# A third attention head transposed in squares by VectorE, with its stores and buffers rearranged

## The chip, the core and the metric

The kernel runs on one core of a Trainium2 chip. The metric is the device time of one execution in microseconds (us). A core has TensorE (PE, matrix products; its weight loads are PEld), VectorE (DVE), ScalarE (ACT), GpSimd (POOL) and SyncE (SP), each with its own instruction queue in program order. They wait for one another by semaphores. Data moves between main memory, the on-chip memory SBUF and within SBUF by DMA; nearly all transfers of this kernel are issued by SP. TensorE writes to PSUM, the accumulators.

## What is computed

A gated block on 8 sequences of 512 tokens with 512 features: cross attention with 16 heads of 32, then a mixture of 8 experts of which each token takes two, up to 615 tokens an expert. Everything is float32. Cut to what matters:

```python
# x, ctx: (8, 512, 512)
Q = proj(layernorm(x), Wq, bq); K = proj(ctx, Wk, bk); V = proj(ctx, Wv, bv)
attn = softmax(Q @ K^T / sqrt(32))                 # per sequence and head, 512 x 512
x = x + tanh(g_xattn) * ((attn @ V) @ Wo.T + bo)
probs = softmax(layernorm(x) @ Wr + br)            # 8 experts
gates, ids = top_k(probs, 2)
# each expert: its tokens in order of gate, 615 at most
h = silu(xg @ W1 + b1); y = (h @ W2 + b2) * gate
x = x + tanh(g_ffn) * scatter_add(y)
```

The change touches the attention stage only; the expert stage comes after it.

## The kernel before

The attention stage walks over *units* (b, c, qc): batch b (8 sequences), c (4 groups of four heads, for 4 x 32 = 128 rows), and qc (4 tiles of 128 queries). There are 128 units. Four units with the same b and c are called a group here, and the sixteen units of a batch have positions 0 to 15.

A unit is a softmax over 4 heads x 128 queries x 512 keys. `scores` makes the four score tiles in PSUM (`s`, L352) and VectorE takes their maxima (`nm`, L361). `soften` lets ScalarE take the exponentials (L375), which sum themselves. The product with V needs the probabilities with the keys on the partitions, so each head's 128x512 tile has to be transposed. This is done in two ways. Two heads (0 and 1, tile `pr`) are transposed by TensorE, four 128x128 transposes a head (L236, in `turned`), and ScalarE copies the result from PSUM to `p_t` (L395). The other two (2 and 3, tile `by_part`) are first moved by four DMAs a unit, one for each block of 32 key positions (L380), into the tile `laid_p`; there VectorE transposes 32x32 squares straight into `p_t` (L405, in `turn_laid_heads`).

The loop over units is a hand-made pipeline, and every engine keeps its written order (the scheduler is manual):

```python
for n, u in enumerate(units):
    loads(b, c, qc)
    ps, nm = scores(nxt)
    # pre: norms' statistics and rows, routing steps
    # at qc == 0: weighted(previous c), the product with V
    turn_heads(u)
    soften(nxt, ps, nm)
    # main: one projection; at qc == 0: divide
    # more: turning of rows, router
    turn_laid_heads(u)
```

So in the iteration of unit u the scores of the next unit come first, then the TensorE transposes of u, the exponentials and laid transfers of the next unit, one projection (q at qc 0, k at 1, v of the next batch at 2, the output projection of the batch before at 3; `pj`, L300), and VectorE's squares of u come last. `weighted` (L423, `po`) needs all four heads' `p_t` of the four units; `divide` (L442, `o_t`) multiplies `po` by the reciprocal sums, which TensorE spreads (`pt_r`, L436) and ScalarE copies (`over`, L438).

The tables `pre`, `main` and `more` put the work of the norms and the router at fixed positions (`put`, `put_ln2`). `ln1_stats`, `ln1_apply` and `ln1_turn` prepare a tile of 128 tokens of the next batch: `bn_stats` on VectorE, the normalized rows `xn` (L229), and their transposition. `ln2_stats`, `ln2_apply` and `ln2_turn` do it for the second norm, after the output projection. `ln2_apply` also issues the stores of the token tile: its residual rows to `out_x` (L261) and its normalized rows to `xn_rows` (L262), from which the experts gather. As `pre` stands ahead of `soften`, these two stores stand ahead of that iteration's four laid transfers in SP's queue.

The pools decide how many tiles of a name are alive: `xn` has 3 buffers, the token tiles `x_1` (first norm) and `x_2` (residual) have 4 each, `by_part`, `laid_p`, `pr` have 2. The two score tiles of a unit use all of the score buffers, so the scores of the unit after next wait for the exponentials of the next one.

## Time and profile before

| what | value |
|---|---|
| time, median of 3 executions | 2032.08 us (2031.86 to 2032.39) |
| the profiled execution | 2030.15 us |
| its span, first to last instruction | 2028.4 us |
| mean granted TensorE clock in it | 0.977 of full speed |

By stretches of that execution:

| stretch (us) | what runs | PE busy | DVE busy | ACT busy | PE clock | DMA share |
|---|---|---|---|---|---|---|
| 0 to 29 | loads, first projections | 29.00 | 8.26 | 7.24 | 1.00 | 0.83 |
| 29 to 142 | batch 0 | 105.41 | 65.78 | 69.92 | 0.97 | 0.40 |
| 142 to 851 | batches 1 to 6 | 697.00 | 470.93 | 446.10 | 1.00 | 0.41 |
| 851 to 967 | most of batch 7 | 109.96 | 72.00 | 68.00 | 0.91 | 0.35 |
| 967 to 1080 | end of attention, first routing | 76.18 | 73.99 | 23.45 | 0.79 | 0.33 |
| 1080 to 2028 | experts | 923.70 | 589.64 | 238.82 | 0.99 | 0.43 |

How to read such views. A row of a group of instructions gives the line, engine, operation, the tiles (written <- read) and shapes, how often it ran, its busy time in total and the mean of one in ns, and the idle time of its engine just before it with what ended that idle time. A timeline gives start and length of merged instructions in order of time. Matmuls are recorded twice here (a float32 product of 512 columns appears as two records), and their ends are modelled. The granted clock is what the chip's throttle let TensorE have.

### The profile page before, as it was taken

How to read it: one execution, taken by the hardware profiler on the slowest of the kernel's cores; microseconds unless marked ns; L12 is line 12 of the kernel's file. 1: busy time of each engine (PE TensorE's matmuls, PEld its weight loads, DVE VectorE, ACT ScalarE, POOL GpSimd, SP SyncE). 2: the span in 40 equal slices, each digit the busy share in tenths (PEclk: the TensorE clock that was granted, in tenths of full speed). 3: DMA queues.
4: the chain of work that ended last, by engine and by line, in shares of the span. 5: the costliest groups of instructions: out<-in, count | busy, mean ns of one | idle time of the engine just before them, and what ended most of it. 6: DMA issues, size and time to landing. Idle time of an engine off the chain costs nothing.

```text
span 2028.4 us, 27201 instructions
## 1 busy us (share of the span) xinstructions
PE 1930.5 (95%) x8784; PEld 1151.1 (57%) x8784; DVE 1279.6 (63%) x2693; ACT 851.8 (42%) x2014; POOL 603.5 (30%) x798
## 2 busy tenths in 40 slices
PE   7989999999999999998669999999999999999997
PEld 3334444444444444444346777777777777777775
DVE  3566666667666666766568675776767667772540
ACT  3656667566666756565213032230403223041321
POOL 1001110010111001110135463536545365464533
PEclk9999999999999999998779999999999999999998
DMA  7243434434343443333511545344553534455332
GB/s 259 74 116 90 128 110 120 125 94 139 104 123 110 121 124 96 103 114 89 150 51 52 157 88 135 89 114 117 110 148 87 138 89 111 124 113 136 88 68 26
DMA packets 291678, 224.58 MB, mean 111 GB/s; under 512 B 26768, under 2 KB 260944, under 8 KB 291536
## 3 DMA queue, kind: packets, MB, share of 16 engines
q1 hardware_dynamic: 282704, 201.96, 35.7%
q0 software_dynamic: 8832, 20.88, 5.6%
q8 instruction: 71, 1.16, 0.3%
q14 instruction: 71, 0.58, 0.1%
HBM read 107.75 MB, written 29.77 MB: 68 GB/s over the span
## 4 chain that ended last, share of the span: by engine, by line
PE 73%; DVE 8%; ACT 7%; DMA 4%; issue 4%; SPq 2%; POOL 1%; POOLq 0%; ACTq 0%; DVEq 0%
PE ps L933 40%; PE pj L300 13%; PE po L423 6%; PE s L352 6%; PE pt L236 5%; ACT by_part L375 3%; DVE nm L361 2%; ACT pr L375 2%; DMA laid_p<-by_part 2%; DVE p_t L405 1%; DMA w<-in_W 1%; SPq L874 1%; SPq L380 1%; DVE ht L917 1%; ACT q_t L309 1%
## 5 line engine op out<-in xcount | busy, mean ns | idle before, releaser
L361 DVE TENSOR_REDUCE nm<-s 128x2 f32<-128x1024 f32 x256 | 298.1, 1204 | 52.6 <-PE s L352 52.5
L395 ACT COPY p_t<-pt 128x512 f32<-128x512 f32 x256 | 138.1, 589 | 276.7 <-PE pt L236 276.5
L933 PE MATMUL ps<-xg_t,w 128*128 128x308 f32 x768 | 220.1, 423 | 0.5 <-ACT u L986 0.5
L223 POOL TENSOR_TENSOR rstd<-rstd,nhalf 128x1 f32<-128x1 f32 x64 | 37.0, 578 | 613.9 <-DVE rstd L222 613.9
L352 PE MATMUL s<-k_t,q_t 32*128 32x512 f32 x1024 | 193.9, 653 | 25.4 <-ACT by_part L375 17.8
L933 PE MATMUL ps<-h,w 128*128 128x308 f32 x768 | 207.5, 425 | 0.0
L375 ACT ACTIVATE by_part<-s,nm 128x512 f32<-128x512 f32 x256 | 174.5, 691 | 53.1 <-DVE nm L361 47.8
L933 PEld LDWEIGHTS ps<-xg_t,w 128*128 128x128 f32 x768 | 145.8, 190 | 53.9 <-ACT u L986 1.0
L375 ACT ACTIVATE pr<-s,nm 128x512 f32<-128x512 f32 x256 | 174.4, 697 | 0.0
L933 PEld LDWEIGHTS ps<-h,w 128*128 128x128 f32 x768 | 143.7, 190 | 52.6 <-issue 3.2
L236 PEld LDWEIGHTS pt<-ident,pr 128*128 128x128 f32 x1024 | 112.5, 143 | 103.4 <-issue 100.3
L405 DVE STREAM_TRANSPOSE p_t<-laid_p 128x512 f32<-128x512 f32 x256 | 165.9, 686 | 5.0 <-DMA laid_p<-by_part 4.7
L933 PE MATMUL ps<-tg,s1w 128*128 128x308 f32 x512 | 145.3, 426 | 9.3 <-ACT p1s L961 5.5
L442 DVE TENSOR_TENSOR o_t<-po,over 128x512 f32<-128x512 f32 x32 | 22.1, 691 | 207.3 <-ACT over L438 207.3
L236 PE MATMUL pt<-ident,pr 128*128 128x128 f32 x1024 | 143.4, 284 | 2.7 <-ACT pr L375 2.7
L423 PE MATMUL po<-p_t,v_s 128*32 128x512 f32 x1024 | 142.4, 628 | 0.9 <-DVE p_t L405 0.9
L933 PE MATMUL ps<-ht,s2w 128*128 128x308 f32 x512 | 137.9, 426 | 0.0
L957 ACT ACTIVATE h<-c,b 128x308 f32<-128x308 f32 x192 | 101.4, 549 | 74.3 <-DVE c L996 72.1
L933 PEld LDWEIGHTS ps<-tg,s1w 128*128 128x128 f32 x512 | 94.9, 190 | 52.8 <-issue 20.5
L300 PE MATMUL pj<-ctx_t,wk 128*128 128x512 f32 x256 | 117.0, 600 | 7.1 <-DMA ctx_t<-in_ctx_t 7.1
L933 PEld LDWEIGHTS ps<-ht,s2w 128*128 128x128 f32 x512 | 95.5, 190 | 34.8 <-issue 1.8
L300 PE MATMUL pj<-xn_t,wq 128*128 128x512 f32 x248 | 111.6, 592 | 0.0
(191 smaller groups left out, 3105.0 us busy)
## 6 DMA issues: line engine op xcount, KB each, us to landing
laid_p<-by_part SPq DMA_DIRECT2D x512, 128.0 KB
w<-in_W SPq DMA_DIRECT2D x128, 256.0 KB
w<-in_W SPq DMA_DIRECT2D x64, 512.0 KB
x<-in_x SPq DMA_DIRECT2D x64, 256.0 KB
laid<-xg SPq DMA_DIRECT2D x140, 64.0 KB
out_x<-x SPq DMA_DIRECT2D x32, 256.0 KB
xn_rows<-xn SPq DMA_DIRECT2D x32, 256.0 KB
ctx_t<-in_ctx_t SPq DMA_DIRECT2D x28, 256.0 KB
```

Of the source, the lines that this page charges most:

```text
L223: nc.gpsimd.tensor_tensor(rstd, rstd, nhalf, ALU.pow)
L236: nc.tensor.transpose(pt[:, c, :], src[:, c * P : (c + 1) * P], ident)
L300: nc.tensor.matmul(ps, lhsT=lhs(ic), rhs=rhs(ic), start=(ic == 0), stop=(ic == DC - 1))
L352: nc.tensor.matmul(ps[i // 2][:, i % 2, :], lhsT=q_t[b, c][r, cols(qc)], rhs=k_t[b, c][r, :], start=True, stop=True,)
L361: nc.vector.tensor_reduce(nm[:, 2 * i : 2 * i + 2], ps[i], AX.X, ALU.max, negate=True)
L375: nc.scalar.activation(to, of, AF.Exp, bias=nm[:, i : i + 1], accum_out=sums[b, c][:, qc, i : i + 1])
L395: nc.scalar.copy(p_t[b, c][i][:, :, cols(qc)].rearrange("p c (q j) -> p c q j", q=DC), pt.rearrange("p c (j q) -> p c q j", q=DC),)
L405: nc.vector.transpose(p_t[b, c][i][:, :, cols(qc)].rearrange("p c (q j) -> p q c j", q=DC), laid[:, :, i - 2].rearrange("p q (c i) -> p q ...
L423: nc.tensor.matmul(po[i * HD : (i + 1) * HD, :], lhsT=v_s[b][:, kc, h * HD : (h + 1) * HD], rhs=pts[i][:, kc, :], start=(kc == 0), stop=(k ...
L442: nc.vector.tensor_tensor(o_t[b][:, c, :], po, over, ALU.mult)
L933: nc.tensor.matmul(ps, lhsT=lhs[k], rhs=rhs[k], start=(k == 0 and not onto), stop=(k == n - 1), skip_group_check=onto,)
L957: nc.scalar.activation(hh[q, i], src, AF.Silu, bias=b1[:, j : j + 1])
```

## The change

It does three things. The second head of `pr` joins the laid path: `by_part` and `laid_p` carry three heads (LH = 3), `pr` one, the exponentials run in the order 2, 3, 1, 0, and VectorE transposes three heads a unit. The two stores of a token tile leave `ln2_apply` and become `ln2_store`, put into `more` at the same position, so after `soften`. And room is made: `xn` has 2 buffers for 3 and `x_1` has 3 for 4; the fourth `x_1` tile of a batch is loaded three units later, and in the first batch it takes an `x_2` buffer.

```diff
+LH = 3
...
-        def load_x(b, j, use):
-            t = acts.tile([P, D], F32, tag=f"x_{use}", name=f"x_{use}", bufs=4)
+        def load_x(b, j, use, of=None):
+            of = of or use
+            t = acts.tile([P, D], F32, tag=f"x_{of}", name=f"x_{of}", bufs=2 + of)
...
-            xn = probs.tile([P, D], F32, tag="xn", name="xn", bufs=3)
+            xn = probs.tile([P, D], F32, tag="xn", name="xn", bufs=2)
...
         def ln2_apply(b, j):
-            t = b * TT + j
             xn = norm_apply((2, b, j))
-            nc.sync.dma_start(out=out[t * P : (t + 1) * P, :], in_=x_in.pop((2, b, j)))
-            nc.sync.dma_start(out=xn_rows[t * P : (t + 1) * P, :D], in_=xn)
             rows_n[2, b, j] = xn
+
+        def ln2_store(b, j):
+            r = slice((b * TT + j) * P, (b * TT + j + 1) * P)
+            nc.sync.dma_start(out=out[r, :], in_=x_in.pop((2, b, j)))
+            nc.sync.dma_start(out=xn_rows[r, :D], in_=rows_n[2, b, j])
...
-            by_part = probs.tile([P, DC, 2, P], F32, tag="by_part", name="by_part")
-            p_sb[u] = probs.tile([P, 2, S], F32, tag="pr", name="pr")
-            for i in (2, 3, 0, 1):
+            by_part = probs.tile([P, DC, LH, P], F32, tag="by_part", name="by_part")
+            p_sb[u] = probs.tile([P, S], F32, tag="pr", name="pr")
+            for i in (2, 3, 1, 0):
...
-            laid_p[u] = probs.tile([P, DC, 2, P], F32, tag="laid_p", name="laid_p")
+            laid_p[u] = probs.tile([P, DC, LH, P], F32, tag="laid_p", name="laid_p")
...
-            pr = p_sb.pop(u)
-            for i in range(2):
-                pt = turned(pr[:, i, :])
-                nc.scalar.copy(
-                    p_t[b, c][i][:, :, cols(qc)].rearrange("p c (q j) -> p c q j", q=DC),
-                    pt.rearrange("p c (j q) -> p c q j", q=DC),
-                )
+            pt = turned(p_sb.pop(u))
+            nc.scalar.copy(
+                p_t[b, c][0][:, :, cols(qc)].rearrange("p c (q j) -> p c q j", q=DC),
+                pt.rearrange("p c (j q) -> p c q j", q=DC),
+            )
...
-            for i in range(2, QH):
+            for i in range(LH):
                 nc.vector.transpose(
-                    p_t[b, c][i][:, :, cols(qc)].rearrange("p c (q j) -> p q c j", q=DC),
-                    laid[:, :, i - 2].rearrange("p q (c i) -> p q c i", c=DC),
+                    p_t[b, c][1 + i][:, :, cols(qc)].rearrange("p c (q j) -> p q c j", q=DC),
+                    laid[:, :, i].rearrange("p q (c i) -> p q c i", c=DC),
                 )
...
             put(pre, b_at, t + 2, ln2_apply, b, j)
+            put(more, b_at, t + 2, ln2_store, b, j)
...
+            if (c, qc) == (0, 3) and b + 1 < B:
+                load_x(b + 1, 3, 1)
...
                 if b + 1 < B and c == 0:
-                    for j in range(2, TT):
-                        load_x(b + 1, j, 1)
+                    load_x(b + 1, 2, 1)
...
             for j in range(TT):
-                load_x(0, j, 1)
+                load_x(0, j, 1, 1 + j // 3)
```

## The prediction

> **What bounds the kernel now.** I read the page's busy times first, then TensorE's clock and busy time by stretches, then the timeline of one group of four units queue by queue, then the waits of VectorE and of SP. On the page, TensorE is busy almost throughout; the three rows that the change moves work between stand below it. Columns are: busy time in total, mean of one in ns, idle time before it.
>
> ```profile
> PE 1930.5 (95%) x8784; PEld 1151.1 (57%) x8784; DVE 1279.6 (63%) x2693; ACT 851.8 (42%) x2014; POOL 603.5 (30%) x798
> ...
> L395 ACT COPY p_t<-pt 128x512 f32<-128x512 f32 x256 | 138.1, 589 | 276.7 <-PE pt L236 276.5
> ...
> L405 DVE STREAM_TRANSPOSE p_t<-laid_p 128x512 f32<-128x512 f32 x256 | 165.9, 686 | 5.0 <-DMA laid_p<-by_part 4.7
> ...
> L236 PE MATMUL pt<-ident,pr 128*128 128x128 f32 x1024 | 143.4, 284 | 2.7 <-ACT pr L375 2.7
> ```
>
> The share of 95% tempts one to price the change as TensorE work saved. The timeline shows that two places of each group are not TensorE's. It is one group (c=0 of batch 4), TensorE, VectorE and ScalarE; columns are start and length in us, then idle time before it.
>
> ```profile
> 503.00 1.20 PE L352 MATMUL s<-k_t,q_t 32*128 32x512 f32 x8
> 504.13 4.62 PE L423 MATMUL po<-p_t,v_s 128*32 128x512 f32 x32
> 508.68 1.09 PE L236 MATMUL pt<-ident,pr 128*128 128x128 f32 x8
> 509.61 3.60 PE L300 MATMUL pj<-xn_t,wq 128*128 128x512 f32 x8
> ...
> 513.58 1.14 PE L352 MATMUL s<-k_t,q_t 32*128 32x512 f32 x8
> ...
> 519.48 1.13 PE L352 MATMUL s<-k_t,q_t 32*128 32x512 f32 x4 [0.30 <-ACT by_part L375]
> 520.81 1.13 PE L352 MATMUL s<-k_t,q_t 32*128 32x512 f32 x4 [0.21 <-ACT pr L375]
> ...
> 526.77 1.14 PE L352 MATMUL s<-k_t,q_t 32*128 32x512 f32 x8
> ...
> 503.78 1.29 DVE L405 STREAM_TRANSPOSE p_t<-laid_p 128x512 f32<-128x512 f32 x2
> ...
> 514.88 0.69 DVE L442 TENSOR_TENSOR o_t<-po,over 128x512 f32<-128x512 f32 x1 [6.40 <-ACT over L438]
> 515.49 1.29 DVE L405 STREAM_TRANSPOSE p_t<-laid_p 128x512 f32<-128x512 f32 x2
> 516.71 2.32 DVE L361 TENSOR_REDUCE nm<-s 128x2 f32<-128x1024 f32 x2
> ...
> 517.98 0.69 ACT L375 ACTIVATE by_part<-s,nm 128x512 f32<-128x512 f32 x1 [1.56 <-DVE nm L361]
> ```
>
> First place: po started at 504.13 and took 4.62; another (534.97 to 538.54, not shown) takes 3.57. The extra 1.05 is head 3's square transposes, which VectorE starts only at 503.78, after it has emptied the projection. Second place: the scores at 519.48 waited, and their second half at 520.81 waited again. Followed back: exps from 517.98, maxima from 516.71, transposes from 515.49, o_t from 514.88. So the periods between scores are 10.58, 5.90, 7.29 and 7.13 us (starts 503.00, 513.58, 519.48, 526.77, 533.90; the last holds 1.0 of the router).
>
> The clock by stretches (us, PE, PEld, DVE, ACT and POOL busy, granted clock, DMA share, GB/s): a stretch with only 1.68 of 3.50 us busy is followed by one at half clock; the emptiest steady stretch, 2.89 busy, is not.
>
> ```profile
> 85.00:88.50 3.50, 1.68 (x10) 0.61 (x8) 2.82 (x4) 3.17 (x10) 0.00 (x0) 1.00 0.07 24
> 89.10:92.50 3.40, 3.40 (x18) 0.78 (x20) 2.52 (x3) 0.00 (x0) 0.00 (x0) 0.50 0.47 101
> 518.80:522.20 3.40, 2.89 (x12) 0.93 (x12) 3.13 (x8) 2.54 (x7) 0.55 (x1) 1.00 0.42 153
> ```
>
> And the waits of VectorE and SP (total, times, longest):
>
> ```profile
> DVE p_t L405 <- DMA laid_p<-by_part: 4.7, 4, 3.3
> SPq L262 <- DVE xn L229: 102.2, 26, 5.4
> ```
>
> VectorE hardly waits for the transfers, so there is slack in them; SP stands 102 us behind the norm's rows, and nobody waits for SP.
>
> **What the Trainium skill says.** "TensorE: Matmul & The Clock Gate", Part 1: The HAM clock gate, says that the array's clock halves after an idle window of 3413 ns on a free-running timer. The trace agrees on the length (half clock from 89.1 for 3.4 us) but a half-empty window was enough. "VectorE: DVE Perf Modes", The three transpose paths: VectorE transposes only 32x32 blocks; the trace has the price here, 686 ns for 128x512. "DMA: Bandwidth & Descriptors", Issuing engines are not separate DMA queues: transfers of all queues interleave on the same 16 engines, so larger laid transfers can delay others; the trace has them busy at 0.41 to 0.42 in steady batches, which leaves room.
>
> **The change, part by part.** (1) Removed per unit: four TensorE transposes and one ScalarE copy. Eight transposes run from 508.68 to the product after them in 1.02 us, so four are 0.51; x128 = 65 us. The copies are 128 x 0.589 = 75 us, off the path. (2) Added per unit: one VectorE transpose. Two take 1.22 until the next instruction starts (515.49 to 516.71), so a third adds 0.61; x128 = 78 us. (3) The laid transfers grow from 128 to 192 KB each, four per unit, and start one exp (0.67) later. In the chain of waits one lands 3.01 us after its issue (512.48 to 515.49), and SP issues the four in 2.49 (511.88 on, 1.49 after the first exp at 510.39): the last lands 7.0 after the first exp, and with 0.67 and an estimated 0.15 for the bytes 7.8. The transposes that need them come 9.55 after it in a short case (523.52 to 533.07): hidden, with 1.7 to spare. Without that cover each unit would pay the excess.
>
> Now the path, by place in the group. *First unit (qc 0):* po needs the last head's square, 0.61 later; the turn after it is 0.51 shorter. Sum +0.10. *Second:* the chain o_t, transposes, maxima, exps gets 0.61 longer and TensorE has 0.51 less to do meanwhile: +0.61, all as idle TensorE. *Third:* its scores' second half comes 1.34 after the first as before; then the turn is 0.51 shorter: -0.51. *Fourth:* -0.51; the maxima move 0.61 later, but their exps end at 6.1 and the scores after them are shadowed by po's wait. Sum -0.31 a group, x32 = -10 us.
>
> Given back: at positions 9 to 11 of a batch VectorE also carries a bn_stats set (1.09), a norm (0.45) and choose_largest (0.95). Its transposes then end 0.5 to 0.6 later in the next unit, and the scores' second half at 11 waits 0.97 that it did not: +1.0 in each of five batches (2 to 6). At position 3 the stats ahead of the emptying and a TensorE shorter by 0.51 take the cover from position 4's po (it had about 0.6): +0.4 to 0.6 in seven batches. Position 5 gives -0.1, since two turns there fill its wait. In all +8 to +9: the chain comes out at -1 us.
>
> (4) Stores behind the unit's transfers: out_x and xn_rows leave pre and go after soften, so four laid transfers pass two stores and the xn wait; loads of later iterations are still behind them. No engine waited there (VectorE's 4.7 above), so 0; if the cover of (3) were gone it would be worth up to 0.33 + 0.34 us of issue in 32 units, some 20 us at most. (5) xn 3 to 2 buffers, x_1 4 to 3, and one x load three units later: at most two xn are alive, a norm at position 6 takes the buffer turned at 5, and x_1's fourth tile takes the one read at position 2 before its load at 3. The load is read at 9. Cost 0; upper end one store's landing, estimated 3 us x 28 = 84, excluded unless the trace shows xn waiting. (6) The tail: three transposes instead of two before the last product, 0.61 - 0.51; 0.
>
> (7) The clock, which the trace of before shows only at the start and tail. In the second unit TensorE's product now ends at 5.02 (5.19 as modelled), the scores start at 6.51, and their halves leave 0.21 between: 1.54 idle of 3.41, so 1.87 busy. Falls followed 1.68 (of 3.50), 1.62 (of 3.50, 142.90 on) and 1.97 (115.80 to 119.20); 2.00 (54.90 to 58.30) had none. So the new hole lies just below the line. The windows that hold enough of it start within about 0.97 us of 3.41: a chance of 0.28. Position 5 is filled by turns, so three groups a batch count; leaving out those near falls that exist already, 20 x 0.28 = 5.6 falls, each 3.41/2 = 1.7 less 0.1 slack: +9 us. Bounds: 0 if the line is lower, and some 32 us if each of 20 falls.
>
> Sum: the profiled span 2028.4 - 1 + 9 = 2036.4; that execution lasted 2030.15, 1.75 around the span, and the median is 1.93 above it. So 2032.1 + 8 = 2040.
>
> **Rivals.** *A, forecast (0.51): chain even, clock falls.* 2034 to 2050, likeliest 2040. *B (0.21): chain even, clock stays.* 2031, 2028 to 2036. For it: the 2.89 row and only four falls in 1000 us; against it: the hole triples. *C (0.22): faster.* VectorE's extra work at positions 3 and 9 to 11 hides (their engines are not saturated), the clock stays: -10 us, 2022, down to 2012 if SP's earlier transfers also help. Its deciding point is the idle before the second unit's scores: below about 1 us of it, C wins. *D (0.06): transfers late.* 50% more bytes; each unit's transposes would wait, 0.2 us x 128 = +26, 2058. Against it: the 1.7 us to spare. The full 65 us of TensorE (1967) would need VectorE's chain out of the path; the two waits at 519.48 and 520.81 exclude it.
>
> **The numbers.** Time 2040. Range 2021 to 2052: it leaves out half of D, the far ends of C and A. The likeliest case's own range is 2034 to 2050. A measurement of this kernel can tell 0.2%, 4 us, from no change: faster 0.24 (C and a little of B), same 0.24 (B and A's near end), slower 0.52.
>
> **What would show it.** Right: periods near 10.6, 6.5, 6.8; an idle of 1.3 to 1.5 us before half of the second units' scores; po's wait 1.6 instead of 1.0; several half-clock stretches between 164 and 930 us. Wrong: p_t waiting for laid_p (D), a period of 5.9 kept in the second place (C), or xn waiting for a store.

## The result, and the profile after

The changed kernel takes 2111.59 us (median of 4 executions, 2107.14 to 2113.77) against 2032.24 us for the kernel before on the same chip: a ratio of 1.0387, interval 1.0369 to 1.0405. It is slower, as forecast, but by 79 us where the prediction had 8, and the time lies far outside its range of 2021 to 2052. The batches of attention take 124 to 133 us instead of 118 (from the scores of a batch's second unit to those of the next batch's). In the table of stretches of the kernel before, the first row (0 to 29 us) has the columns of other engines: TensorE, VectorE and ScalarE were busy for 18.28, 7.24 and 5.49 us there; nothing rests on it.

The page of the changed kernel, with the rows that answer to those of before: busy time by engine, the granted clock and the DMA engines' share in 40 slices (tenths), the hardware queue (packets, MB, share of the 16 engines' span), and three rows of groups (busy in total, mean in ns, idle before them).

```profile
PE 1955.7 (93%) x8272; PEld 1128.4 (53%) x8272; DVE 1356.8 (64%) x2821; ACT 790.0 (37%) x1886; POOL 603.7 (29%) x798
...
PEclk9888999999999999999678999999999999999998
DMA  8676867777877777777841244544353444535331
...
q1 hardware_dynamic: 282704, 235.51, 53.2%
...
L407 DVE STREAM_TRANSPOSE p_t<-laid_p 128x512 f32<-128x512 f32 x384 | 242.4, 682 | 65.6 <-DMA laid_p<-by_part 64.0
...
L397 ACT COPY p_t<-pt 128x512 f32<-128x512 f32 x128 | 75.0, 586 | 325.1 <-PE pt L238 325.1
```

Two things stand out. VectorE's squares now wait 64.0 us for their transfers, against 4.7 before. And the DMA row: during attention the engines are mostly 60 to 80% busy (before: 30 to 40%), though the queue moved only 17% more bytes (235.51 MB against 201.96). TensorE has 512 instructions fewer, exactly those that the change removes, and still is busy for 25 us more: part of its time ran at half clock.

One group of the changed kernel (c=0 of batch 4), TensorE and VectorE; start and length in us, then idle time before it.

```profile
541.46 1.14 PE L356 MATMUL s<-k_t,q_t 32*128 32x512 f32 x8
...
542.76 1.90 DVE L407 STREAM_TRANSPOSE p_t<-laid_p 128x512 f32<-128x512 f32 x3 [0.94 <-DMA laid_p<-by_part]
...
544.58 2.32 DVE L365 TENSOR_REDUCE nm<-s 128x2 f32<-128x1024 f32 x2
...
547.35 1.13 PE L356 MATMUL s<-k_t,q_t 32*128 32x512 f32 x4 [0.72 <-ACT by_part L379]
...
548.69 1.13 PE L356 MATMUL s<-k_t,q_t 32*128 32x512 f32 x4 [0.21 <-ACT pr L379]
549.14 1.90 DVE L407 STREAM_TRANSPOSE p_t<-laid_p 128x512 f32<-128x512 f32 x3 [1.59 <-DMA laid_p<-by_part]
...
549.74 4.97 PE L425 MATMUL po<-p_t,v_s 128*32 128x512 f32 x32
...
565.60 1.13 PE L356 MATMUL s<-k_t,q_t 32*128 32x512 f32 x4 [1.33 <-DVE xn L231]
...
566.93 1.13 PE L356 MATMUL s<-k_t,q_t 32*128 32x512 f32 x4 [0.21 <-ACT pr L379]
...
568.50 5.28 PE L304 MATMUL pj<-wv,ctx_t 128*128 128x512 f32 x8
```

Read it from the top. The squares at 542.76 waited 0.94 us for a transfer, so the maxima behind them (544.58) and the exponentials were late, and the scores at 547.35 waited. The squares at 549.14 waited 1.59, and po, which began at 549.74, took 4.97 instead of 4.62. The second unit's scores at 565.60 and 566.93 waited 1.33 + 0.21 = 1.54 us (they do not read `xn`, which the row names; they wait for the exponentials to free their buffer): this is the predicted hole to the hundredth. Right after it a product that takes 3.60 elsewhere takes 5.28, at half clock.

The waits of the whole execution of the changed kernel (total us, times, longest):

```profile
DVE p_t L407 <- DMA laid_p<-by_part: 64.0, 44, 5.0
...
ACT by_part L379 <- DMA laid_p<-by_part: 25.8, 11, 2.7
```

The second line is all but new (0.3 us before): exponentials of a unit wait until the transfers of two units earlier have read their buffer. SP's wait for the norm's rows (102.2 us before) has shrunk to 7.5 us, and nobody gains from that.

### The profile page after: what moved, and what is told of

The parts are those of the page before. It is cut to its first block, busy times and chain, and to the rows that moved or that the text cites. A ratio compares the mean times of both kernels' runs of the same rounds, so it can differ in the third digit from the quotient of the medians.

```text
span 2112.0 us, 25980 instructions
## 1 busy us (share of the span) xinstructions
PE 1955.7 (93%) x8272; PEld 1128.4 (53%) x8272; DVE 1356.8 (64%) x2821; ACT 790.0 (37%) x1886; POOL 603.7 (29%) x798
## 3 DMA queue, kind: packets, MB, share of 16 engines
q1 hardware_dynamic: 282704, 235.51, 53.2%
## 4 chain that ended last, share of the span: by engine, by line
PE 61%; DVE 11%; DMA 11%; ACT 9%; SPq 4%; issue 3%; POOL 0%; DVEq 0%; POOLq 0%; ACTq 0%
PE ps L938 37%; PE pj L304 9%; DMA laid_p<-by_part 8%; PE po L425 7%; ACT by_part L379 5%; PE s L356 4%; DVE p_t L407 4%; SPq L384 3%; PE pt L238 2%; DVE nm L365 2%; ACT q_t L313 1%; DMA w<-in_W 1%; SPq L879 1%; DVE ht L922 1%; ACT pr L379 1%
## 5 line engine op out<-in xcount | busy, mean ns | idle before, releaser
L379 ACT ACTIVATE by_part<-s,nm 128x512 f32<-128x512 f32 x384 | 259.3, 686 | 143.9 <-DVE nm L365 111.0
L356 PE MATMUL s<-k_t,q_t 32*128 32x512 f32 x1024 | 226.0, 673 | 73.3 <-ACT by_part L379 44.5
L407 DVE STREAM_TRANSPOSE p_t<-laid_p 128x512 f32<-128x512 f32 x384 | 242.4, 682 | 65.6 <-DMA laid_p<-by_part 64.0
L397 ACT COPY p_t<-pt 128x512 f32<-128x512 f32 x128 | 75.0, 586 | 325.1 <-PE pt L238 325.1
L425 PE MATMUL po<-p_t,v_s 128*32 128x512 f32 x1024 | 164.3, 653 | 12.8 <-DVE p_t L407 12.2
L356 PEld LDWEIGHTS s<-k_t,q_t 32*128 32x128 f32 x1024 | 62.6, 190 | 168.8 <-ACT by_part L379 96.9
L304 PE MATMUL pj<-wv,ctx_t 128*128 128x512 f32 x240 | 126.8, 678 | 0.0
L425 PEld LDWEIGHTS po<-p_t,v_s 128*32 128x32 f32 x1024 | 58.1, 118 | 118.3 <-issue 51.3
L238 PEld LDWEIGHTS pt<-ident,pr 128*128 128x128 f32 x512 | 57.3, 148 | 107.3 <-issue 103.5
```

Of the source, the lines that this page charges most:

```text
L238: nc.tensor.transpose(pt[:, c, :], src[:, c * P : (c + 1) * P], ident)
L304: nc.tensor.matmul(ps, lhsT=lhs(ic), rhs=rhs(ic), start=(ic == 0), stop=(ic == DC - 1))
L356: nc.tensor.matmul(ps[i // 2][:, i % 2, :], lhsT=q_t[b, c][r, cols(qc)], rhs=k_t[b, c][r, :], start=True, stop=True,)
L379: nc.scalar.activation(to, of, AF.Exp, bias=nm[:, i : i + 1], accum_out=sums[b, c][:, qc, i : i + 1])
L397: nc.scalar.copy(p_t[b, c][0][:, :, cols(qc)].rearrange("p c (q j) -> p c q j", q=DC), pt.rearrange("p c (j q) -> p c q j", q=DC),)
L407: nc.vector.transpose(p_t[b, c][1 + i][:, :, cols(qc)].rearrange("p c (q j) -> p q c j", q=DC), laid[:, :, i].rearrange("p q (c i) -> p q ...
```

## The experiments

Three theories were tested. *Chain*: the longer VectorE chain of each group's second unit, with the clock's falls that its hole brings (the forecast). *Bytes*: the 192 KB transfers come late (the prediction's rival D). *Stores*: the stores and buffers cost something. Ratios are to the kernel before on the same chip; a clock fall is a stretch at half clock that begins between 150 and 920 us of the profile. In most runs the first of them, between 150 and 166 us, comes at the end of batch 0, where the kernel before has one too (at 147).

| run | what it is | time (us) | ratio, 95% interval | falls |
|---|---|---|---|---|
| after | the change | 2111.59 | 1.0387 (1.0369 to 1.0405) | 14 |
| e1 | three heads' squares, two heads' bytes | 2065.16 | 1.0167 (1.0138 to 1.0195) | 17 |
| e2 | two heads' squares, three heads' bytes | 2071.99 | 1.0191 (1.0165 to 1.0217) | 4 |
| e3 | after, destination pitch 2048 B | 2107.57 | 1.0369 (1.0343 to 1.0395) | 9 |
| e4 | after, rows of 2048 B | 2281.75 | 1.1224 (1.1191 to 1.1258) | 21 |
| e5 | before, with the stores and buffers of after | 2032.29 | 1.0008 (0.9997 to 1.0019) | 1 |
| e6 | e1 with unread products in the hole | 2037.92 | 1.0035 (1.0020 to 1.0049) | 1 |
| e7 | after, context's load in parts | 2100.73 | 1.0346 (1.0328 to 1.0363) | 11 |
| e8 | e7 with unread products in the hole | 2098.35 | 1.0335 (1.0318 to 1.0352) | 6 |
| e9 | before, first unit's squares later | 2006.71 | 0.9863 (0.9828 to 0.9897) | 2 |
| e10 | e9, context's load in parts | 2008.22 | 0.9882 (0.9862 to 0.9902) | 2 |
| e11 | e10 with three heads everywhere | 2074.74 | 1.0213 (1.0196 to 1.0230) | 6 |
| e12 | e10 with three heads in first units only | 1999.05 | 0.9842 (0.9825 to 0.9859) | 2 |
| e13 | after, rows split, SP issues | 2078.11 | 1.0235 (1.0211 to 1.0258) | 17 |
| e14 | after, rows split, POOL issues the third head's | 2070.56 | 1.0186 (1.0160 to 1.0212) | 19 |
| e15 | e11, rows split, SP issues | 2022.08 | 0.9956 (0.9942 to 0.9970) | 1 |
| e16 | e11, rows split, POOL issues the third head's | 2026.98 | 0.9976 (0.9957 to 0.9994) | 5 |
| e17 | after, eight transfers of 96 KB | 2149.99 | 1.0588 (1.0561 to 1.0615) | 16 |
| e18 | before, transfers over two queues | 2033.41 | 1.0005 (0.9992 to 1.0018) | 3 |

### The parts of the change: e1, e2, e5

Diffs of e1 and e2 are against after, that of e5 against before.

```diff
# e1: third head's exponentials aside, its squares read a head that was moved
-            for i in (2, 3, 1, 0): ... to = by_part[:, :, i - 1, :]
+                if i == 1: to = aside
+                elif i:    to = by_part[:, :, i - 2, :]
-                    laid[:, :, i]
+                    laid[:, :, max(i - 1, 0)]
# e2: turn_heads and two squares of before, rows of three heads
+            by_part = by_parts[units.index(u) % 2]       # third head zeros
-            for i in range(LH):
+            for i in range(2):
# e5: before, with
+            put(more, b_at, t + 2, ln2_store, b, j)
+            xn: bufs=2; x_1: bufs=3; load_x(b + 1, 3, 1) at (0, 3)
```

> The changed kernel with laid transfers of two heads (128 KB) as before: head 1's exponentials go to a tile that nobody reads, and VectorE's third transpose reads head 2's squares again, so head 1's share of the output is computed from head 2's. VectorE's chain, the shorter TensorE work, the store order and the buffers are all as in the change; only the bytes are not. Theory T (the larger transfers cost the time: they land 6.3 us after the first issue instead of 4.2): the time falls to what the prediction had for chain and clock, 2030 to 2048 us, p_t waits under 8 us for laid_p. Theory V (VectorE's chain and the falling TensorE clock cost it, the transfers only follow): it stays above 2085 us.

> The changed kernel with the heads divided as before (two transposed by TensorE, two by VectorE), but with the laid transfers of three heads' size, 192 KB; the third slot carries zeros. Stores and buffers as in the change; the reciprocal sums share a buffer with pr to make room. The transfers start one exp earlier than in the change. Theory T: slower than before by 10 to 40 us, with the last packet 6 us or more after the first issue, and p_t or by_part waiting for laid_p. Theory V: within 4 us of 2032.

> The change without its third head: two heads by TensorE and two by VectorE with transfers of 128 KB as before, but the stores behind the unit's transfers, xn with 2 buffers, x_1 with 3 and the later x load. If stores and buffers cost nothing, as the prediction had it: 2028 to 2036 us. If the rest between the two runs so far (79 us against 34 and 41 for chain and bytes) is theirs: 2036 to 2045.

e5 is settled: stores and buffers cost nothing that can be measured. e1 lies between its two brackets and e2 just above the 10 to 40 us of its first; each costs about half of the whole, so both other theories hold something. In e2, by the mean periods between scores, the loss sits mostly at position 12 (14.48 us against 10.31 in the mean of six batches, 25 us in these); position 0 has 0.4 more, most others within 0.2. The transfers of the unit before it stand behind the 1 MB load of the next context, which is issued at position 10, and the squares in the iteration of position 11 begin 9.8 us after its scores instead of 6.5. Elsewhere e2's transfers just make it: it issues them after two exponentials, the changed kernel after three.

### What the packet's size does: e3 and e4

The packets of the laid transfers had a median of 46 ns in the kernel before (rows of 1024 B) and 154 ns in the changed one (1536 B), by the profile's packets from 280 to 930 us. e3 leaves the row and changes the destination's pitch; e4 moves four heads' worth.

```diff
# e3
-            laid_p[u] = probs.tile([P, DC, LH, P], ...)
+            laid_p[u] = probs.tile([P, DC, LH + 1, P], ...)
-    out=laid_p[u][rows].rearrange("p q h k -> p (q h k)")
+    out=laid_p[u][rows, :, :LH].rearrange("p q h k -> p q (h k)")
# e4: the same tile, and a source row of LH + 1 heads, which overlaps its neighbour
+    in_=by_part.rearrange("p g h k -> p (g h) k")[:, g * LH - g // LH : ... + LH + 1]
```

> The changed kernel, all of its work, but laid_p's rows lie 2048 bytes apart instead of 1536; each row of a transfer still carries 1536 bytes. If the slow transfers come from where the rows land (a pitch that is no power of two), packets fall from 152 ns towards 65 and the time to 2030 to 2050 us. If they come from the length of a row or from its source, packets stay near 150 ns and the time near 2111. Theory V: 2111 whatever the packets do.

> The changed kernel with laid rows of 2048 bytes: every transfer carries four heads' length (256 KB), 512 bytes of it from the next block and unused, and laid_p's rows lie 2048 bytes apart; one of the four key blocks arrives shifted by a head, so the output differs there. If 1536 bytes is a bad length, packets of 2048 take about 84 ns, as the x loads' do, the last lands about 5 us after the first issue, and the time is 2030 to 2055 us in spite of more bytes. If the bytes themselves are the cost, it is slower than the change, above 2130. Theory V: 2111.

The pitch is not it: e3's packets stay at 153 to 158 ns. e4 shows that more bytes cost more: its last transfer lands 8.5 us and more after the unit's first issue, and the time is far above everything else.

### The clock: e6

```diff
# e6: e1, with, at the end of each second unit's iteration
+                if qc == 1:
+                    fill = ps_t.tile([P, DC, P], F32, tag="pt", name="fill")
+                    for _ in range(6):
+                        nc.tensor.matmul(fill[:, 0, :], lhsT=ident, rhs=ident, start=True, stop=True)
```

> The run with VectorE's third transpose and transfers of two heads (2065 us), with six products of the identity that nobody reads put on TensorE at the end of each second unit's iteration, some 1.3 us that fall into its hole. Theory C (the falls of the clock make all of the 34 us, and the chain itself comes out even): no half-clock stretch between 160 and 880 us, the third unit's period back from 8.5 to 6.9, the time 2024 to 2040 us. Theory V (VectorE's chain is the cost, the clock only follows): 2060 us or more, since TensorE only gets more to do.

Three stretches around a second unit's scores in e1 (us, busy time of PE, PEld, DVE, ACT and POOL, granted clock, DMA share, GB/s):

```profile
660.55:663.95 3.40, 3.40 (x10) 1.34 (x8) 3.40 (x6) 0.59 (x1) 0.00 (x0) 1.00 0.16 24
663.95:667.40 3.45, 1.92 (x9) 0.60 (x8) 3.35 (x7) 3.36 (x9) 0.55 (x1) 1.00 0.13 45
667.40:670.80 3.40, 3.40 (x10) 1.59 (x7) 3.40 (x5) 1.36 (x4) 0.00 (x0) 0.50 0.93 255
```

And a second unit in e6:

```profile
642.40:645.80 3.40, 3.19 (x20) 1.94 (x20) 3.31 (x7) 2.98 (x9) 0.40 (x1) 1.00 0.08 30
645.80:649.20 3.40, 3.40 (x13) 1.61 (x14) 3.40 (x5) 1.73 (x5) 0.15 (x1) 1.00 0.85 221
```

In e1 a stretch with 1.92 of 3.45 us busy is followed by one at clock 0.50. With the hole filled the clock stays, 17 falls become 1 (the one at the end of batch 0), and the time goes from 2065.16 to 2037.92: the falls were worth 27 us. What is left of the chain, with the filling itself, is 0.35%, 7 us: nearly even, as the prediction's sum of -1 had it.

"TensorE: Matmul & The Clock Gate", Part 1: The HAM clock gate, of the Trainium skill says that the window is free-running. The trace agrees: the falls of e1 begin on one grid of 3.413 us. Seven of them (483.1, 513.8, 544.5, 575.2, 606.0, 636.7 and 667.4 us) are 30.7 apart, which is nine windows. Four batches of e6 take 117.9 us, so a group takes 29.5; a fall adds up to 1.7 and makes it about as long as those nine windows. That a group which is caught therefore hands the next one to the same place of a window is a reading of these distances, and no run tests it. The forecast of 5.6 falls was too low for another reason too.

The prediction drew its line from windows that end 0.6 to 0.7 us before the half clock begins. In windows that end where it begins, busy time draws no line. In the kernel before the clock fell at 119.82 and not at 58.38 us:

```profile
116.41:119.82 3.41, 2.59 (x12) 0.76 (x16) 1.65 (x4) 2.37 (x7) 0.00 (x0) 1.00 0.34 113
54.97:58.38 3.41, 1.93 (x16) 1.27 (x12) 3.41 (x5) 2.21 (x5) 0.00 (x0) 1.00 0.39 81
```

In e1 it fell at 483.09 and not at 756.15 us:

```profile
479.68:483.09 3.41, 2.43 (x10) 0.85 (x11) 3.18 (x11) 2.63 (x8) 0.56 (x2) 1.00 0.27 92
752.74:756.15 3.41, 2.09 (x7) 0.73 (x7) 3.41 (x5) 1.85 (x5) 0.00 (x0) 1.00 0.00 0
```

The busy time of the first of these two is nearly all score products, which work on 32 partitions (`32*128` in their rows), that of the second mostly a projection on 128. Over all 20 profiles there are 4201 windows at full clock between 165 and 915 us, 138 of them followed by a fall. The best line in busy time puts 85 of them on the wrong side. With score products counted at 0.4 of their time, a line at 1.42 us has 8 on the wrong side. Slid over e1's timeline, windows under that line give 13 falls by chance and windows under the prediction's 1.98 give 5; 16 were measured after batch 0 (changed kernel: 14 by chance against 13, e14: 14 against 18). This is an estimate made afterwards, from modelled ends, and no run tests it.

### The context's load, and late transfers in general: e7 and e8

```diff
# e7: after, with the 1 MB load in four parts, one each at positions 10 to 13
-            if (c, qc) == (2, 2) and b + 2 < B:
-                load_ctx(b + 2, DC)
+            if b + 2 < B and 10 <= c * TT + qc < 10 + DC:
+                ctx_part(b + 2, c * TT + qc - 10)
# e8: e7 with the filling of e6
```

> The changed kernel with the next context's load spread over positions 10 to 13, a quarter of 256 KB each, instead of 1 MB at position 10. Theory P (the larger laid transfers cost time only at positions 11 and 12, where they queue behind that load): position 12 goes from 13.5 to about 10.3 and the time from 2111 by 20 to 35 us to 2076 to 2091. If the bytes cost in every unit: above 2100.

> The changed kernel with both: the context's load spread and TensorE's hole in the second unit filled. If collision (P) and clock (C) are the whole of the loss: 2026 to 2045 us, which is what the prediction gave for an even chain. If there is a third cause: above 2055.

Both times fell to the rival in their expectations: e7 is just above 2100, as if the bytes cost in every unit, and e8 is above 2055, which meant a third cause. The load was worth 11 us (position 12 fell from 13.47 to 11.31 us). The filling was worth next to nothing, but only halved the falls, from 11 to 6. e8 has e6's chain, and differs by the bytes, the exponential that the transfers now wait for, and the load in parts; yet it takes 60 us more, and its batches 124 to 128. So the theory that the bytes only cost where they meet the load had fallen. The waits of e8 from 280 to 930 us show what is in the way:

```profile
ACT by_part L385 <- DVE nm L371: 78.3, 42, 2.6
...
DVE p_t L413 <- DMA laid_p<-by_part: 35.8, 39, 1.6
ACT by_part L385 <- DMA laid_p<-by_part: 24.9, 10, 2.7
```

In e6 the same stretch has the squares waiting once:

```profile
ACT by_part L382 <- DMA laid_p<-by_part: 15.4, 15, 1.1
...
DVE p_t L410 <- DMA laid_p<-by_part: 1.0, 1, 1.0
```

Of the 39 short waits 16 are of third units' squares, which makes the fourth's maxima late, and 20 of fourth units', for which the next po waits: the mean period of the group's first place is 1.0 to 2.0 us longer than e6's, that of the fourth up to 0.8.

Where the time goes was then read from packets and issues, as medians over six batches. Before: the first transfer is issued 1.49 us after a unit's first exponential has begun, the last lands 4.0 us after that. After: 2.14, and 6.36. In e1, with the old bytes: 1.47 and 4.0. The squares that wait begin some 1.24 us after the last landing (e8; half of them between 1.0 and 1.4).

### Moving the squares instead: e9 to e12

The hole of the second unit comes from the first unit's squares, which stand between o_t and the maxima. They are needed only by the next po. e9 turns them an iteration later, and e10 to e12 build on it.

```diff
# e9, against before (e11 and e12: with three heads)
                 ps, nm = scores(nxt)
+                if qc == 1:
+                    turn_laid_heads(units[n - 1])
...
-                turn_laid_heads(u)
+                if qc:
+                    turn_laid_heads(u)
# e10, e11, e12: also the load in parts, as e7
# e12: three heads only where qc == 0
+            lh = 3 if qc == 0 else 2
```

> The kernel before (two heads' squares), with one edit: the squares of each group's first unit are turned by VectorE an iteration later, behind the maxima of the third unit instead of ahead of those of the second unit's successor. Theory (the second unit's scores wait for o_t, then squares, then maxima, then exps, all on VectorE and ScalarE): the second period loses its 0.5 us of idle TensorE, 5.90 to about 5.4, in 32 groups: 2032 - 16 = 2016 (2008 to 2022). Rival (VectorE merely does the same work 5 us later and holds the third unit up instead): the third period grows by what the second loses, 2028 to 2045.

> The run with the late squares, with the 1 MB load of the next context in four parts over positions 10 to 13. Theory (with 128 KB transfers the load delays nobody who is needed): within 4 us of the run with late squares alone. Rival (the load already costs the kernel before something at position 12, whose period is 10.31 against 10.1): 1 to 5 us faster than it.

> The changed kernel (three heads' squares, 192 KB transfers) with late squares and with the context's load in parts. Theory (most of the change's loss is that 192 KB land 2 us later than 128 KB, and that third and fourth units then wait; the late squares take the second unit's hole and with it the clock's falls away, but leave the other three units' transfers as late as they are): 2060 to 2090, batches of 121 to 124 us. Rival (the loss is the longer VectorE chain of the second unit and its hole): the chain is out of the path here, and 0.51 us of TensorE in each unit shows: below 2025.

> As the run with late squares, load in parts and three heads, but three heads only in each group's first unit, whose squares are late and have some 5 us more until they are needed; the other three units keep two heads and 128 KB. Theory (192 KB cost only where they are needed within about 8 us of the first issue): the third head is free here and saves TensorE 0.51 us a group: 16 us below the run with late squares and spread load, about 2000 (1993 to 2012). Rival (more bytes cost wherever they are moved, since all transfers share the engines): the same as that run or slower, 2012 to 2030.

A second unit in e9:

```profile
503.94 1.14 PE L352 MATMUL s<-k_t,q_t 32*128 32x512 f32 x8
...
505.24 0.69 DVE L442 TENSOR_TENSOR o_t<-po,over 128x512 f32<-128x512 f32 x1 [6.40 <-ACT over L438]
...
505.85 2.35 DVE L361 TENSOR_REDUCE nm<-s 128x2 f32<-128x1024 f32 x2
...
508.11 1.29 DVE L405 STREAM_TRANSPOSE p_t<-laid_p 128x512 f32<-128x512 f32 x2
...
509.47 1.65 PE L352 MATMUL s<-k_t,q_t 32*128 32x512 f32 x8
...
510.87 1.30 DVE L405 STREAM_TRANSPOSE p_t<-laid_p 128x512 f32<-128x512 f32 x2
```

The maxima follow o_t at once, and the period is 5.53 instead of 5.90 (509.47 - 503.94). The third place gains more: 7.22, 7.14, 7.29 and 7.29 before, 6.40, 5.99, 6.48 and 6.47 in e9. Its period begins with the scores that waited. In the kernel before they came as two halves (519.48 and 520.81), each of which took 1.13, and 2.39 us passed until the next instruction of TensorE (521.87); in e9 all eight take 1.65, and 1.58 pass (to 511.05). The difference of 0.81 is what most third places gained. In all the time falls by 25 us, more than the 16 expected. Spreading the context's load adds nothing here (e10). TensorE is then busy for all but half a us in 450 (stretch from 280 to 730 us, columns as above):

```profile
280.00:730.00 450.00, 449.49 (x2339) 218.85 (x2339) 312.58 (x523) 290.24 (x710) 48.61 (x68) 1.00 0.43 121
```

The kernel before has 443.79 there at full clock, the changed one, whose TensorE has less to do:

```profile
280.00:730.00 450.00, 422.43 (x1887) 185.78 (x1888) 316.86 (x522) 239.27 (x596) 41.81 (x59) 0.97 0.78 140
```

Only now is TensorE the bound, and only now does its work count. e11 has the whole of the change's saving of TensorE and no hole, and stays at 2074.74, 67 us slower than e10. e12 takes the saving where the squares have five more us, and is 9 us faster than e10 (the intervals of the ratios, 0.9825 to 0.9859 and 0.9862 to 0.9902, just part). It is the fastest of all, 1.6% below the kernel before, though e9 alone can't be told from it.

### Why 192 KB land so late: e13 to e18

First the same bytes as a row of 1024 B and one of 512 B:

```diff
# e13 (e15: on e11); e14 and e16 have nc.gpsimd in the second loop
             for g in range(DC):
                 nc.sync.dma_start(out=laid_p[u][rows of g], in_=by_part[:, g])   # two heads
+            for g in range(DC):
+                nc.sync.dma_start(out=one[rows of g], in_=by_one[:, g])           # the third
...
-            for i in range(LH):
+            for i in (1, 2, 0):
                 nc.vector.transpose(
```

> The changed kernel, with each unit's 192 KB as four transfers of 128 KB (rows of 1024 B, heads 2 and 3, issued after the second exp as before) and four of 64 KB (rows of 512 B, head 1), all from SP; VectorE turns head 1 last. Row theory (rows above 1024 B are what is slow): packets of 1024 B back near 46 to 60 ns, VectorE's waits for the transfers of heads 2 and 3 gone, what is left are the clock's falls and SP's four more issues (2.5 us a unit): 2050 to 2085. Byte theory (the bytes themselves cost): packets of 1024 B near 100 ns, 2095 to 2115 as the changed kernel.

> As the run with split rows, with POOL issuing the four transfers of head 1 in place of SP. Row theory: 2045 to 2080, no later than with SP alone, unless POOL's own issues are slow. Byte theory: 2095 to 2115. If POOL's issues take it over 1 us each, the gates and norms on POOL are late and both are spoilt: above 2115.

> Late squares, context's load in parts, three heads, and the rows split with SP issuing all. Row theory: the waits of 2074.74 go, and three heads' saving of TensorE shows: 1975 to 2010. Byte theory: 2060 to 2080, as unsplit. Between (2010 to 2060): head 1's transfers, which SP issues last, are late themselves.

> As the run before it, with POOL issuing head 1's transfers. Row theory: 1970 to 2005. Byte theory: 2060 to 2080. Above 2080: POOL's issues are the cost.

From 280 to 930 us, the queue of the changed kernel and its laid transfers (packets, MB, share of the engines):

```profile
q1 hardware_dynamic: 64012, 90.26, 77.3%
...
laid_p<-by_part SPq DMA_DIRECT2D x332, 192.0 KB
```

and that of e13:

```profile
q1 hardware_dynamic: 114225, 92.46, 51.5%
...
laid_p<-by_part SPq DMA_DIRECT2D x336, 128.0 KB
laid<-by_one SPq DMA_DIRECT2D x340, 64.0 KB
```

The same bytes in twice the packets keep the engines busy for two thirds of the time. Packets of 1024 B are back at 46 ns, those of 512 B take 27, together 73 where one of 1536 B took 154. The time falls by 33 us (e13 against after) and by 53 us (e15 against e11). e13 and e14 lie in the brackets of the row theory, e15 between the two, and e16 22 us above its bracket and 33 below the other. The squares' waits in the same stretch, first e11:

```profile
DVE p_t L413 <- DMA laid_p<-by_part: 38.3, 28, 3.2
```

then e15:

```profile
DVE p_t L421 <- DMA laid_p<-by_part: 1.5, 1, 1.5
DVE p_t L421 <- DMA laid<-by_one: 0.2, 1, 0.2
```

With the waits go the 53 us, which shows late transfers as their cause.

This looked like a proof that rows above 1024 B are slow. But in the changed kernel the packets of each unit's first transfer take 65 ns during its first 0.3 us, and only from about 0.6 us on, when SP has issued the next, 150 to 210. Two more runs were to tell length from overlap:

```diff
# e17, against after: each transfer as two of 64 rows of 1536 B
+                for r in range(2):
+                    nc.sync.dma_start(out=laid_p[u][16 partitions], in_=by_part[r * 64 : (r + 1) * 64, g])
# e18, against before: 1024 B, every second transfer from ScalarE's queue
-                nc.sync.dma_start(
+                (nc.scalar if g % 2 else nc.sync).dma_start(
```

> The changed kernel with each of a unit's four 192 KB transfers issued as two of 96 KB (64 rows of 1536 B each); SP issues eight, 0.62 us apart. Overlap theory (transfers that are not done when the next begins slow each other): each is done in about 0.3 us, so packets take a median of 65 ns, the queue's share of the engines falls from 77% to about 40 to 50%; the eighth issue comes 4.4 us after the first, so the last lands 6.4 to 6.8 us after it, and the time stays at 2090 to 2120. Length theory (a row above 1024 B is slow in itself): packets 120 ns and more, share above 65%, time 2110 to 2150.

> The kernel before (rows of 1024 B, 128 KB transfers), with the second and fourth transfer of each unit issued by ScalarE's queue in place of SP's. Overlap theory: two are in flight at once, packets rise from a median of 46 ns to 80 ns and more, and the queues' share of the engines from 40% to 55% or more. Length theory: 46 ns and 40% as before. The time says little (2025 to 2060), since ScalarE pays for the issues and the transfers have time in hand.

The same stretch of e17:

```profile
q1 hardware_dynamic: 66559, 86.60, 48.5%
```

and of e18, which has two queues:

```profile
q1 hardware_dynamic: 43056, 49.66, 32.2%
q10 hardware_dynamic: 25344, 23.08, 18.9%
```

As to packets, overlap it is: the long rows of e17 take a median of 65 ns, the short ones of e18 take 86, and the share rises from 40.0% to 51.1%. But packets that are shorter by half did not bring the last landing forward. The landings, medians over six batches, with the first packet 1.21 us after the first issue in each (e14: in the units where POOL begins 0.94 us after SP):

| run | KB a unit, rows | last issue | last lands | rate from the first packet |
|---|---|---|---|---|
| before | 512, 1024 B | 1.90 | 4.01 us | 524 KB / 2.80 us = 187 GB/s |
| e18 | 512, 1024 B, two queues | 0.61 | 4.00 us | 188 GB/s |
| after | 768, 1536 B | 1.90 | 6.36 us | 786 KB / 5.15 us = 153 GB/s |
| e17 | 768, 1536 B, halves | 4.42 | 6.62 us | 145 GB/s |
| e13 | 768, 1024 and 512 B | 4.48 | 6.08 us | 161 GB/s |
| e14 | 768, the third head's issued by POOL | 2.60 | 5.33 us | 191 GB/s |

e18 issues all four within 0.61 us instead of 1.90, and they land no sooner. So already in the kernel before earlier issues would have brought nothing: 512 KB took 2.8 us of moving either way. In e17 and e13 the rate says something else. There SP issues the last of eight transfers 4.4 to 4.5 us after the first, and 1.21 later its first packet can move; the last landing comes only 1.0 (e17) and 0.4 us (e13) after that. These two were paced by SP.

e14 was not, since POOL issued the third head's transfers beside SP's. There 768 KB took 4.12 us of moving, 191 GB/s (55 of the 83 units with all packets on record; over all 83 it is 4.41 us, 178 GB/s). So three heads' bytes can go at about the rate of two heads', and need 1.3 to 1.6 us more than these. The rest of the 2.35 us by which the changed kernel's transfers land later, 0.7 to 1.0, belongs to how they are cut or issued: to rows of 1536 B, to transfers that overlap or to the single queue, which no run separates. A packet's time and the share of the engines count packets that wait for each other (stretches of the changed kernel show shares above 1), and so say little about the rate.

What then made e13 and e15 faster? By the records, order: in e13 heads 2 and 3 are issued after two exponentials again (1.48 us after the first began, against 2.14; in e15 about half of the units, the others later) and land 4.01 us later, and the third head's, which lands 6.08 after the first issue, is turned last, 1.2 us after the squares began. The squares of heads 2 and 3 so have 0.66 + 2.35 = 3.0 us more, the last square 0.66 + 0.28 + 1.2 = 2.1. No run tested this order without the split.

e17's time missed the overlap theory's 2090 to 2120 and lies at the end of the length theory's 2110 to 2150 (2149.99), though its packets, share and landing are those of overlap. SP spends 5.0 us of each unit on issues instead of 2.5. That everything else which it moves is late for this, and makes the time, is a reading.

"DMA: Bandwidth & Descriptors", Why small descriptors are slow (HBM only), of the Trainium skill says that transfers from SBUF to SBUF don't suffer from small descriptors. Packets that hardly wait for each other do not quite agree: those of 512, 1024 and 1536 B take 27, 46 and 65 ns (e13, the kernel before, e17), so short ones take longer for a byte. What that does to a landing no run shows.

## Why the prediction was wrong

**Right.** Step 1: 512 instructions of TensorE and half of ScalarE's copies went. Step 2: three squares take 1.82 us to the next instruction (542.76 to 544.58) against 1.22: +0.60, predicted 0.61. The path's second place: period 6.49, predicted 6.51, with idle times of 1.33 and 0.21. Third place without a fall, in e1: 6.86, predicted 6.78. The chain's sum of -1: e6 has +7 with its filling. Steps 4 and 5: nothing (e5). That the 65 us of TensorE wouldn't come, since it wasn't the bound at the two waits: e9 shows it from the other side.

**Wrong, step 3: "the last lands 7.0 after the first exp, and with 0.67 and an estimated 0.15 for the bytes 7.8".** The 7.0 was read from a chain that ends with squares at 515.49. These turn the unit before, not the one whose transfers were issued at 511.88, and had not waited. By the packets the last lands 1.49 + 4.01 = 5.5 us after the first exponential, and a square that waits can begin at 6.7. The 0.67 was right (2.14 - 1.49 = 0.65). The 0.15, for which no working is given, counts next to nothing for the bytes, as if only the issues set the landing. They didn't: 50% more bytes took 6.36 - 4.01 = 2.35 us more, of which 1.3 to 1.6 are moving at about the old rate (e14). By the same counting, instead of 7.8, the squares can begin 2.14 + 6.36 + 1.24 = 9.7 us after the first exponential, where 9.55 is when a short unit needs them: the "1.7 to spare" was nothing, and third and fourth units paid. The step that failed is that term: 0.15 for the bytes, where 2.35 was measured. A wait of 4.7 us in the whole profile said that there was slack, not how much the bytes would use. Rival D named the mechanism with 0.06 and priced it at 26 us. The context's load, behind which the larger transfers are late by microseconds, was in neither; spreading it gave 11 us (e7).

**Too small, step 7: "20 x 0.28 = 5.6 falls", +9 us.** That the hole makes the clock fall was right, and so was the hole (1.87 busy predicted, 1.92 of 3.45 in the window of e1). The chance wasn't: 16 falls after batch 0, and 27 us (e1 against e6), near the upper bound of 32 that the text gave. The step that failed is the line at 1.97 to 2.00 us of busy time, from which the chance of 0.28 follows: of e1's 16 falls 9 came after windows with 1.87 to 1.89 us busy, and 7 after windows with 2.08 to 2.57. By the estimate above, places drawn by chance make 13 falls with a better line and 5 with that one. Whether the places are also tied to one another, so that the rest is no chance, stays open.

**The sum as measured**, in steps of one part each: before 2032; the chain with its falls 2065 (e1, +33, of which the falls 27); the third head's bytes, issued behind the other two heads', 2078 (e13, +13); all three heads in one transfer, issued an exponential later, 2112 (+33). They aren't independent: e8, which halves the falls, spreads the load and leaves the late transfers, gains only 13 of the 79, since units that wait for transfers have other holes and other periods. e1 and e2, at +33 and +40, come near the whole, but no run shows that they add up.

**Open.** What limits these transfers to 191 GB/s at most, and what the changed kernel's way of cutting or issuing them costs beyond that. Whether issuing heads 2 and 3 first is all that e13 gained. Whether a group that is caught by the clock's window hands the next one to the same place, and whether score products count for less in it: both are read from profiles, and no run shifted the windows or changed the products.

## What to carry to other kernels

Ask of a transfer whether its landing is set by the issues or by the rate: the landing of all of a unit's transfers after the first issue, not the wait of who reads them, tells how much 50% more bytes cost. Before moving work off a busy engine, see which wait ends last at the places where it is idle; here the reordering of two steps on VectorE gave 25 us, and only behind it, and where the transfer had time, was the saved TensorE work worth something. Before a chance is worked out from a line in busy time, try the line on all windows of a profile, each ending where the recorded clock can change, and see whether it divides them; where it doesn't, give the bound instead of the chance.

## What was not expected of the hardware

- Transfers from SBUF to SBUF that move 128 rows into 32 partitions went at 188 GB/s at most for 512 KB, no faster from two queues than from one, and at 153 (one queue) and 191 GB/s (two queues, e14) for 768 KB. A unit's first rows went faster: in the changed kernel 125 of 512 within 0.6 us of the first packet (median).
- A packet took 46 ns or 86 (1024 B, before and e18), 65 or 154 (1536 B, e17 and after), with the landing of the last no different within each pair by more than 0.3 us.
- The clock fell after windows with 1.88 us of 3.41 busy, but also after some with 2.4 to 2.6, and stayed after some with 1.93 and 2.09 (rows above); score products seem to count for less than half of their time (an estimate from 138 falls). In e1 six distances in a row between falls were 30.7 us, nine windows.
